# Attention steps taken in pairs, runs in another order, and the instruction order laid out nine times

## The chip, the core and the metric

The kernel runs on one core of one Trainium2 chip. The core has TensorE (matmuls, "PE" in the profile, its weight loads "PEld"), VectorE ("DVE"), ScalarE ("ACT"), GpSimd ("POOL") and SyncE ("SP"), which issues the DMAs. The metric is the device time of one execution in microseconds (us); lower is better.

## The reference

Two layers work on x of shape (2, 1024, 512), all in fp32. Each layer normalises x and adds to it causal attention and a gated feed-forward network of the same normalised input:

```python
for layer in range(2):
    xn = layernorm(x)
    x = x + attention(xn, Wq, Wk, Wv, Wo) + ffn(xn, gate, up, down)
# attention: 16 heads of 32; rotary embedding of q and k (two forms); causal softmax(q k / sqrt(32)) v; then Wo
# ffn: (silu(xn gate) * (xn up)) down, hidden 2048 in layer 0, 1408 in layer 1 (there with scales)
```

## The kernel before, in words

**Phases, groups, runs, steps.** There are four phases, one for each layer and batch entry (2 x 2). In a phase the 16 heads form four groups of four heads. A group has four *runs*, one for each block of 256 queries (`qb` 0 to 3); run `qb` has `qb + 1` *steps*, each over 256 keys. So a group has 10 steps, a phase 40, the kernel 64 runs and 160 steps. Runs go in the order 0, 1, 2, 3 in a group, in the last group of all 3, 2, 1, 0 (`blocks_of`).

**One step.** `Run.scores(n)` makes the scores of four heads with 32-row matmuls (`sc` in the profile), four at a time in the array, into two PSUM tiles of the pool `p_st`, each for two heads. That pool has two buffers, so a step's scores fill all of it. ScalarE copies both to SBUF, scaled (`s<-sc`, 1024 columns each; 768 in a run's last step, which leaves out a masked quarter). In the last step `mask` applies the causal mask on GpSimd. `blocks` takes maxima on VectorE (`rmax`). After a run's last step the maxima are transposed on TensorE (`mtr`), written to DRAM and read back spread over all partitions (`md`, `mb`). Then `subtract` (VectorE), `exps` (ScalarE) and `summed` (GpSimd, or VectorE where the list finds it earlier; into `acc`) work on s. `Run.weighted(n)` multiplies the exponentials with the values, in matmuls with 32 output columns (`av`), `Run.total` sums `acc` with a matmul on ones (`av<-acc,ones`), and `normalise` divides on VectorE.

**Kinds of matmul.** The list of the kernel tells three kinds: "full" (128 rows and 128 columns), "rows" (sc) and "columns" (av and totals). All other matmuls are full: the feed-forward's units (`ux`, `uy`, `uz`), the projections of queries, keys and values (the same names with `_qk` and `_v`), the down and output projections (`d`, `ps_o`), transposes (`tr`). [...]

**The loop.** `two_layers` loops over the steps. Step i makes its scores, then runs full work as "fill" (`Fill.run`: a share in units of 0.86 us worth of matmuls, with maxima and exponentials recorded between its pieces), and last multiplies the exponentials of step i - `LAG` (`LAG` is 5) with the values. A finished run's total follows there or just after the next scores. `weight(i)` shares the fill over the steps. `Fill.choose` picks the next piece of fill by what can start; general PSUM results share three banks (`bank`), some of them held by a unit.

**The order.** Calls such as `nc.vector.tensor_tensor` execute nothing at once: `Schedule.record` books an operation with a modelled cost, its dependencies and a modelled start. At the end `emit` calls `again`, which lays all operations out anew: TensorE goes by *pieces* (groups of matmuls that stay together; `next_piece` may put a later full piece first where the next one would wait more than `WAIT`), other engines take the operation that is due first, and leave themselves idle up to `RESERVE` for one that is due soon. The operations are then issued in that modelled order, and each engine works through its own in order. GpSimd's additions may go to VectorE (`either`).

Every recorded operation has the line of the helper (L275) in the profile, so operations are told apart by tile names.

Of the kernel before, what the change touches and what calls it, by code (L numbers as in the profile page):

```python
# [37 lines left out]
LAG = 5  # L38

# [95 lines left out]

class Op:
    __slots__ = ("eng", "call", "deps", "after", "dur", "lat", "seq", "start", "end", "urgent", "table", "ready", "locks", "either", "out", "mode", "late")
# [14 lines left out]
class Schedule:  # L152
# [81 lines left out]
    def record(self, eng, method, args, kwargs):  # L234
# [12 lines left out]
        op.urgent = eng is not self.tensor and any(i.tile.pool.psum in ("m", "av") for i in ins)  # L247
        op.locks = self.locks(eng, method, ins)

        op.either = None  # L250
        if eng is self.gpsimd and method == "tensor_tensor":
            op.either = self.vector, *self.cost(self.vector, method, args, kwargs, outs, ins)
# [19 lines left out]
        def call():  # L272
            target = getattr(getattr(self.nc, op.eng.name), method)
            get = lambda a: a.real() if isinstance(a, View) else a
            target(*[get(a) for a in args], **{k: get(a) for k, a in kwargs.items()})  # L275
# [72 lines left out]
    def emit(self):  # L348
        while any(eng.waiting for eng in self.engines):
            self.give(None)  # L350
        self.again()
        for op in sorted(self.ops, key=lambda op: (op.start, op.seq)):
            op.call()

    def again(self):
# [3 lines left out]
        ops = sorted(self.ops, key=lambda op: (op.start, op.seq))  # L359
        tensor = [op for op in ops if op.eng is self.tensor]  # L360
# [36 lines left out]
        def soonest(op):  # L397

            at = self.tensor.free
            for o in op.deps:  # L400
                if o.start is None:
# [6 lines left out]

        def next_piece():
# [3 lines left out]
            if soonest(pieces[0][0]) <= free + (1000.0 if apart else self.WAIT):  # L413
                return 0
# [17 lines left out]
        for _ in ops:  # L432
            best = None
            for eng in self.engines:
# [4 lines left out]
                if eng is self.vector:  # L439

                    first = min((u for u, _ in can), default=float("inf"))
                    for op in known[self.gpsimd]:
                        if op.either:
                            u = max(self.ready_on(op, eng), eng.free, self.port - self.PORT)
# [38 lines left out]
            if op.eng is not eng:  # L483
                op.eng, op.dur, op.lat = op.either
                op.locks = True
# [10 lines left out]
def two_layers(ctx: ExitStack, tc: tile.TileContext, x_in, attn_w, ffn_w, ffn_s, rope, out):  # L496
# [416 lines left out]
    class Values(Unit):  # L913
# [6 lines left out]
        def __init__(self, ph, pair, begins):  # L920
            self.ph, self.pair, self.name, self.begins = ph, pair, f"_v{ph}_{pair}", begins
# [247 lines left out]
    class Run:  # L1169
# [10 lines left out]
        def scores(self, n):  # L1180
# [18 lines left out]
            for h2 in range(2):  # L1199
                s = self.s[n, h2] = tp.tile([P, 4, 2, P], F32, tag="s", name=f"s{self.name}_{n}_{h2}")  # L1200
                a = 1 if last else 0
                nc.scalar.activation(
                    s[:, a:], st[h2].rearrange("p j b q -> p b j q")[:, a:], AF.Copy, scale=SCALE
                )
# [69 lines left out]
        def summed(self, n, h2):  # L1274

            e = self.s[n, h2].rearrange("p (k b) j q -> p k b (j q)", k=2)
            last = n == self.steps - 1
            if n == 0:
                self.acc[h2] = acc_p.tile([P, 2, 2 * P], F32, tag=f"acc{h2}", name=f"acc{self.name}_{h2}")
            acc = self.acc[h2]  # L1280
            if n == 0 and last:
                nc.gpsimd.tensor_copy(acc[:, 0], e[:, 1, 0])
                nc.gpsimd.tensor_tensor(acc[:, 1], e[:, 0, 1], e[:, 1, 1], ALU.add)
                return
# [9 lines left out]
        def weighted(self, n):  # L1294
            if n == 0:
# [14 lines left out]
        def total(self):  # L1310

            for j in range(HG):
# [28 lines left out]
    def blocks_of(ph, g):  # L1341

        qbs = list(range(NQB))
        return qbs[::-1] if (ph, g) == (len(phases) - 1, NG - 1) else qbs
# [15 lines left out]
    class Fill:  # L1360
# [67 lines left out]
        def late_output(self, step):  # L1428
            for o in self.outs:
                more = any(d[1] == o[1] and d[3] == o[3] for d in self.downs) or (self.later and o[1] == self.ph)  # L1430
                if o[0] <= step and (step - o[0] >= 8 or not more):
# [64 lines left out]
    def queue_phase(ph):  # L1496
# [4 lines left out]
        for g in range(NG):  # L1501
            if g + 1 < NG:
                fill.qk.append((t0 + g * per_group + 1, QueriesKeys(ph, g + 1, t0 + g * per_group + 2)))
# [4 lines left out]
        for pair in range(2):  # L1508
            begins = t0 + 4 + pair
            fill.qk.append((begins - 1, Values(ph, pair, begins)))  # L1510
# [93 lines left out]
    def weight(i):  # L1604
# [3 lines left out]
        return 1.2 if i % per_phase < 10 else 1.0  # L1608

    ended = None  # L1610
    carried = 0.0
    for i in range(total + LAG):
        ph = min(i // per_phase, len(phases) - 1)
        now[0] = i
        if i % per_phase == 0 and i < total:
# [3 lines left out]
        run, n = steps[i] if i < total else (None, 0)  # L1619
        if run:  # L1620
            while turned.get((ph, run.g)) != 4:
                assert fill.run(i - 1, 5.0)
            run.scores(n)
            if ended and ended.acc:
                ended.total()
        old, m = steps[i - LAG] if i >= LAG else (None, 0)
        if run and n == run.steps - 1:
            run.mask(n)

        if ended:  # L1630
            ended.normalise()
            ended = None

        def exponentials(r, k, h2, sums=True):
            r.subtract(k, h2)
            r.exps(k, h2)
            if sums:
                r.summed(k, h2)
            if h2 == 1:
                spread_maxima()  # L1640

        def late(r, k):

            return k == 0 and r.steps == LAG - 1

        between = []
        if old and late(old, m):
            between += [lambda h2=h2: exponentials(old, m, h2) for h2 in range(2)]
        elif old and m == 0:
            for h2 in range(2):  # L1650
                old.summed(0, h2)
        if run:
            between += [lambda h2=h2: run.blocks(n, h2) for h2 in range(2)]
        if 0 <= i - LAG + 1 < total:
            r, k = steps[i - LAG + 1]
            if not late(r, k):

                between += [lambda h2=h2: exponentials(r, k, h2, k > 0) for h2 in range(2)]
        end = total + LAG if ph == len(phases) - 1 else (ph + 1) * per_phase
        share = fill.left((ph + 1) * per_phase) * weight(i) / sum(weight(j) for j in range(i, end))  # L1660
        goal = share + max(-4.0, min(4.0, carried))
        spent = fill.run(i, goal, between)
        while between:
            between.pop(0)()
        transpose_maxima(True)
        if run and n == run.steps - 1:
            found.append(run)
        carried = goal - spent
        if old:
            while (old.ph, 2 * m + 1) not in v:  # L1670
                spent += fill.run(i, 5.0)
                carried = goal - spent
            tiles = [old.s[m, h2] for h2 in range(2)]
            while i < total and spent - goal < 6.0 and max(nc.settled(t) for t in tiles) > nc.tensor.free + SOON:
                more = fill.run(i, 2.0)
                if not more:
                    break
                spent += more
                carried = goal - spent
            old.weighted(m)  # L1680
            if m == old.steps - 1:
                ended = old

                nc.advance(nc.tensor.free)
                if i + 1 >= total or max(nc.settled(acc) for acc in old.acc) <= nc.tensor.free:
                    old.total()
    ended.normalise()
# [58 lines left out]
```

## Time and profile before

| what | value |
|---|---|
| median of three runs | 1841.15 us (1841.02 to 1841.37) |
| the profiled execution | 1841.55 us; span of its instructions 1839.8 us |
| mean granted TensorE clock | 0.999 |
| table loads on ScalarE (exponential, silu, square root) | 168, 215.5 us |
| evictions of scores `s<-sc` on ScalarE | 192 of 1024 columns, 1020 ns; 128 of 768 columns, 806 ns |
| subtractions `s<-s,mb` of 1024 columns on VectorE | 192, mean 1442 ns |

The profile gives, for each group of instructions, its count, the time it kept its engine busy, the mean of one, and the idle time before it with what ended that. The timeline view lists merged instructions in order of time. TensorE's busy time includes the modelled draining of its pipeline, so a rate is read from the distance of two starts.

### The profile page before, as it was taken

To read this page: it belongs to the slowest core of one execution; us is meant where nothing else is said; L and a number is where in the kernel's file an instruction comes from. 1 tells how busy PE (TensorE), PEld (TensorE's weight loads), DVE (VectorE), ACT (ScalarE), POOL (GpSimd) and SP (SyncE) were. 2 spreads that over 40 slices of the span, in tenths; PEclk is the share of its full clock that TensorE was granted. 3 is DMA by queue.
4 is the path that set the end of the run, shared out by engine and by line. 5 is a ranking of instruction groups with operands and counts; after the bars stand their busy time and mean duration, and the time that the engine had idled before them with its cause. 6 is when DMAs were issued, how large, how long until landed. Compare 5 with 4: busy or idle time off the path is not lost.

```text
span 1839.8 us, 25881 instructions
## 1 busy us (share of the span) xinstructions
PE 1815.6 (99%) x9360; PEld 871.5 (47%) x9360; DVE 1518.3 (83%) x2097; ACT 1049.3 (57%) x1251; POOL 1092.0 (59%) x1025
## 2 busy tenths in 40 slices
PE   7999999999999999999999999999999999999998
PEld 3464444444445644444444455444444465444443
DVE  6766987878888668768688888888989998999898
ACT  3444565556556545545574655575565755665762
POOL 5514865656666235545357684866778764667575
PEclk9999999999999999999999999999999999999999
DMA  5325442222232422222222325222223322221101
GB/s 189 95 82 150 133 148 81 70 75 86 70 115 86 129 80 65 75 74 80 70 95 87 121 75 161 75 75 80 70 78 97 112 77 72 63 76 61 58 32 70
DMA packets 140336, 165.16 MB, mean 90 GB/s; under 512 B 13360, under 2 KB 93488, under 8 KB 140208
## 3 DMA queue, kind: packets, MB, share of 16 engines
q1 hardware_dynamic: 140208, 163.50, 28.4%
q8 instruction: 74, 1.21, 0.3%
q14 instruction: 54, 0.44, 0.1%
HBM read 134.62 MB, written 28.84 MB: 89 GB/s over the span
## 4 chain that ended last, share of the span: by engine, by line
PE 93%; DVE 4%; DMA 1%; ACT 1%; issue 1%; POOL 0%; SPq 0%; DVEq 0%; ACTq 0%; POOLq 0%
PE d L275 24%; PE ux L275 19%; PE uy L275 9%; PE av L275 9%; PE sc L275 8%; PE ux_qk L275 5%; PE uz L275 5%; PE ux_v L275 3%; PE uy_qk L275 3%; DVE s L275 2%; PE uy_v L275 2%; PE ps_o L275 1%; PE uz_qk L275 1%; DVE rmax L275 1%; PE tr L275 1%; PE uz_v L275 1%
## 5 line engine op out<-in xcount | busy, mean ns | idle before, releaser
L275 DVE TENSOR_TENSOR s<-s,mb 128x1024 f32<-128x1024 f32 (+2 forms) x448 | 498.6, 1144 | 10.8 <-DMA mb<-md 10.8
L275 POOL TENSOR_TENSOR acc<-acc,s 128x512 f32<-128x512 f32 (+1 forms) x350 | 447.5, 1299 | 52.3 <-ACT s L275 40.5
L275 ACT ACTIVATE s<-sc 128x1024 f32<-128x1024 f32 (+1 forms) x320 | 284.0, 934 | 242.4 <-PE sc L275 226.2
L275 PE MATMUL d<-wd,hT 128*128 128x512 f32 x864 | 401.3, 594 | 0.1
L275 ACT ACTIVATE s<-s 128x1024 f32<-128x1024 f32 (+1 forms) x320 | 303.5, 970 | 167.1 <-DVE s L275 165.2
L275 DVE TRANSPOSE_TENSOR_REDUCE rmax<-s 128x32 f32<-128x1024 f32 (+1 forms) x320 | 350.8, 1117 | 46.6 <-POOL s L275 25.8
L275 POOL TENSOR_TENSOR acc<-s 128x512 f32<-128x512 f32 (+1 forms) x107 | 137.2, 1292 | 248.8 <-PE av L275 163.9
L275 PEld LDWEIGHTS d<-wd,hT 128*128 128x128 f32 x864 | 161.4, 190 | 192.6 <-issue 183.0
L275 ACT ACT_TABLE_LOAD x168 | 215.5, 1283 | 6.7 <-DVE s L275 3.7
L275 DVE TENSOR_TENSOR x<-d,x 128x512 f32<-128x512 f32 x224 | 151.6, 678 | 75.4 <-PE d L275 74.9
L275 POOL TENSOR_SCALAR_AFFINE_SELECT s<-s 128x512 f32<-128x512 f32 x128 | 97.3, 771 | 127.7 <-ACT s L275 124.5
L275 PE MATMUL av<-s,v 128*32 128x256 f32 (+1 forms) x2560 | 159.1, 365 | 2.1 <-DVE oT L275 1.8
L275 PEld LDWEIGHTS av<-s,v 128*32 128x32 f32 x2560 | 67.5, 109 | 144.0 <-issue 97.9
L275 PE MATMUL ux<-xs,wu 128*128 128x512 f32 x212 | 101.7, 602 | 0.1
L275 PE MATMUL ux<-xs,ws 128*128 128x512 f32 x212 | 101.4, 600 | 0.0
L275 PE MATMUL ux<-xnT,wu 128*128 128x512 f32 x212 | 101.3, 600 | 0.0
L275 PE MATMUL uy<-xnT,ws 128*128 128x512 f32 x212 | 99.7, 593 | 1.0 <-ACT p L275 1.0
L275 PE MATMUL ux<-xnT,wg 128*128 128x512 f32 x212 | 100.7, 597 | 0.0
L275 PE MATMUL d<-wo,oT 128*128 128x512 f32 x194 | 100.2, 598 | 0.0
L275 PE MATMUL uy<-xs,ws 128*128 128x512 f32 x212 | 99.7, 593 | 0.4 <-DVE hT L275 0.4
L275 PE MATMUL uz<-xnT,wg 128*128 128x512 f32 x212 | 99.6, 592 | 0.0
L275 ACT ACTIVATE hT<-hT 128x512 f32<-128x512 f32 x62 | 39.1, 630 | 80.7 <-DVE hT L275 80.4
(191 smaller groups left out, 2529.0 us busy)
## 6 DMA issues: line engine op xcount, KB each, us to landing
mb<-md SPq DMA_DIRECT2D x64, 512.0 KB, 3.8
wg<-in_gate SPq DMA_DIRECT2D x54, 256.0 KB, 2.9
wd<-in_down SPq DMA_DIRECT2D x32, 256.0 KB, 3.1
xr<-xm SPq DMA_DIRECT2D x32, 256.0 KB, 2.7
wu<-in_up SPq DMA_DIRECT2D x28, 256.0 KB, 3.0
s12gu<-ws SPq DMA_DIRECT2D x26, 256.0 KB, 2.0
ws<-s12gu SPq DMA_DIRECT2D x26, 256.0 KB, 2.6
wd<-wds SPq DMA_DIRECT2D x22, 256.0 KB, 3.1
```

The costliest lines, as they stand in the source:

```text
L275: target(*[get(a) for a in args], **{k: get(a) for k, a in kwargs.items()})
```

## The change

**Pairs.** The loop goes over pairs of steps (i - 1, i) with i even. A pair first runs a little more fill, up to 6 units, while the exponentials of the first of its two older steps are not nearly ready; then come the scores of step i - 1, the products for steps i - 6 and i - 5 (with totals of runs that end there, or, where `acc` is not ready, after the next scores), the scores of step i, and then the fill of both steps. Maxima of the two new steps and the exponentials of steps i - 4 and i - 3 are recorded between the pieces of that fill.

**Runs in another order.** 2, 0, 1, 3 in a group, 3, 1, 2, 0 in the last. The one-step run (`qb` 0) takes its product's PSUM tile from the general banks, and its total directly from s, with 8 matmuls (4 of 256 columns, 4 of 128), without `acc` on GpSimd.

**Evictions on either engine.** For the first scores of a pair (`soon`) a `tensor_scalar` on VectorE is booked as an alternative to ScalarE's eviction.

**Layouts.** `best` calls `again` for nine pairs of `RESERVE` and `WAIT` and keeps the layout whose last TensorE operation ends first by the model. `next_piece` looks at when the column matmuls of the whole piece can start, not only its first.

**Due times.** The next group's projections of queries and keys come two steps later and open four steps later (order of runs); those of values are queued at steps 1 and 2 of a phase instead of 3 and 4; late output projections are taken after 5 steps instead of 8.

```diff
+PASSES = [(r, w) for w in (300.0, 150.0, 600.0) for r in (600.0, 300.0, 1200.0)]
...
     def emit(self):
         while any(eng.waiting for eng in self.engines):
             self.give(None)
-        self.again()
+        self.best()
...
+        kept, shortest = state(), None
+        for self.RESERVE, self.WAIT in PASSES:
+            self.again()
+            end = max(op.end for op in self.ops if op.eng is self.tensor)
+            if shortest is None or end < shortest:
+                kept, shortest = state(), end
+            else:
+                restore(kept)
...
+        def piece_soonest(piece):
+
+            at, within, inside = soonest(piece[0]), 0.0, set(piece)
+            for op in piece:
+                if op.mode == "columns" and piece[0].mode != "full":
+                    at = max(at, soonest(op, inside) - within)
+                within += op.dur
+            return at
...
-            if soonest(pieces[0][0]) <= free + (1000.0 if apart else self.WAIT):
+            if piece_soonest(pieces[0]) <= free + (1000.0 if apart else self.WAIT):
...
-                    for op in known[self.gpsimd]:
+                    for op in known[self.gpsimd] + known[self.scalar]:
...
-        def scores(self, n):
+        def scores(self, n, soon=False):
...
+                other = ("tensor_scalar", (dst, src, SCALE, None, ALU.mult), {}) if soon else None
+                nc.record(nc.scalar, "activation", (dst, src, AF.Copy), {"scale": SCALE}, other)
...
         def weighted(self, n):
-            if n == 0:
+            if self.steps == 1:
+                self.av = bank(f"av{self.name}", (P, 2, QB))
+            elif n == 0:
                 self.av = p_av.tile([P, 2, QB], F32, tag="av", name=f"av{self.name}")
...
-        qbs = list(range(NQB))
-        return qbs[::-1] if (ph, g) == (len(phases) - 1, NG - 1) else qbs
+        return [3, 1, 2, 0] if (ph, g) == (len(phases) - 1, NG - 1) else [2, 0, 1, 3]
...
-                fill.qk.append((t0 + g * per_group + 1, QueriesKeys(ph, g + 1, t0 + g * per_group + 2)))
+                fill.qk.append((t0 + g * per_group + 3, QueriesKeys(ph, g + 1, t0 + g * per_group + 6)))
...
+    for pair in range((total + LAG + 1) // 2):
+        i = 2 * pair
...
+        new = [(*steps[k], k) for k in (i - 1, i) if 0 <= k < total]
+        old = [steps[k] for k in (i - LAG - 1, i - LAG) if 0 <= k < total]
...
+            while new and more < 6.0 and settled(tiles) > nc.tensor.free + 1200.0:
+                spent = fill.run(i - 1, 2.0)
...
+        scores(i - 1)
+        sums = []
+        for r, m in old:
+            r.weighted(m)
+            if m == r.steps - 1:
 
                 nc.advance(nc.tensor.free)
+                if r.steps == 1 or not new or settled(r.acc) <= nc.tensor.free:
+                    total_of(r)
+                else:
+                    sums.append(r)
+        scores(i)
+        for r in sums:
+            total_of(r)
```

More of the change, by code (lines that the diff above doesn't have):

```diff
@@ L38 @@
 LAG = 5
+LATE = 1.0
 def ts(n, size):
@@ L133 @@
 SOON = 100.0
+PASSES = [(r, w) for w in (300.0, 150.0, 600.0) for r in (600.0, 300.0, 1200.0)]
 class Op:
-    __slots__ = ("eng", "call", "deps", "after", "dur", "lat", "seq", "start", "end", "urgent", "table", "ready", "locks", "either", "out", "mode", "late")
+    __slots__ = ("eng", "call", "deps", "after", "dur", "lat", "seq", "start", "end", "urgent", "table", "ready", "locks", "either", "own", "how", "out", "mode", "late")
 class Engine:
@@ L232, in locks, with record @@
         return eng is self.vector and method == "tensor_tensor" and not any(i.tile.pool.psum for i in ins)
-    def record(self, eng, method, args, kwargs):
+    def record(self, eng, method, args, kwargs, other=None):
         outs = [a for k, a in kwargs.items() if k == "out" and isinstance(a, View)]
@@ L248, in record @@
         op.locks = self.locks(eng, method, ins)
+        op.own = None
         op.either = None
         if eng is self.gpsimd and method == "tensor_tensor":
-            op.either = self.vector, *self.cost(self.vector, method, args, kwargs, outs, ins)
+            op.either = self.vector, *self.cost(self.vector, method, args, kwargs, outs, ins), True, (method, args, kwargs)
+        elif other:
+            op.either = self.vector, *self.cost(self.vector, other[0], *other[1:], outs, ins), False, other
+        op.how = method, args, kwargs
+        if op.either:
+            op.own = eng, op.dur, op.lat, op.locks, op.how
         op.deps, op.after = [], []
@@ L272, in call @@
         def call():
+            method, args, kwargs = op.how
             target = getattr(getattr(self.nc, op.eng.name), method)
@@ L350, in emit, with best, restore @@
             self.give(None)
-        self.again()
+        self.best()
         for op in sorted(self.ops, key=lambda op: (op.start, op.seq)):
             op.call()
+    def best(self):
+        state = lambda: [(op.start, op.end, op.eng, op.dur, op.lat, op.locks, op.how) for op in self.ops]
+        def restore(kept):
+            for op, s in zip(self.ops, kept):
+                op.start, op.end, op.eng, op.dur, op.lat, op.locks, op.how = s
+        kept, shortest = state(), None
[6 more added lines that the diff above has]
+                restore(kept)
     def again(self):
         ops = sorted(self.ops, key=lambda op: (op.start, op.seq))
+        for op in ops:
+            if op.own:
+                op.eng, op.dur, op.lat, op.locks, op.how = op.own
         tensor = [op for op in ops if op.eng is self.tensor]
@@ L395, in again, with soonest @@
         rest, last = [], []
-        def soonest(op):
+        def soonest(op, inside=()):
             at = self.tensor.free
             for o in op.deps:
+                if o in inside:
+                    continue
                 if o.start is None:
@@ L441, in again @@
                     first = min((u for u, _ in can), default=float("inf"))
-                    for op in known[self.gpsimd]:
+                    for op in known[self.gpsimd] + known[self.scalar]:
                         if op.either:
-                            u = max(self.ready_on(op, eng), eng.free, self.port - self.PORT)
+                            u = max(self.ready_on(op, eng), eng.free, self.port - self.PORT if op.either[3] else 0.0)
                             if u + 200.0 < first and u + op.either[2] < self.can_start(op) + op.lat:
@@ L483, in again @@
             if op.eng is not eng:
-                op.eng, op.dur, op.lat = op.either
-                op.locks = True
+                op.eng, op.dur, op.lat, op.locks, op.how = op.either
             self.begin(op, at)
@@ L918, in two_layers, with __init__ @@
         shared = {}
-        def __init__(self, ph, pair, begins):
-            self.ph, self.pair, self.name, self.begins = ph, pair, f"_v{ph}_{pair}", begins
+        def __init__(self, ph, pair, begins, opens):
+            self.ph, self.pair, self.name, self.begins, self.opens = ph, pair, f"_v{ph}_{pair}", begins, opens
         def quarter(self, c, r):
@@ L1201, in scores @@
                 a = 1 if last else 0
-                nc.scalar.activation(
-                    s[:, a:], st[h2].rearrange("p j b q -> p b j q")[:, a:], AF.Copy, scale=SCALE
-                )
+                src, dst = st[h2].rearrange("p j b q -> p b j q")[:, a:], s[:, a:]
+                other = ("tensor_scalar", (dst, src, SCALE, None, ALU.mult), {}) if soon else None
+                nc.record(nc.scalar, "activation", (dst, src, AF.Copy), {"scale": SCALE}, other)
         def mask(self, n):
@@ L1277, in summed @@
             last = n == self.steps - 1
+            if self.steps == 1:
+                return
             if n == 0:
@@ L1280, in summed @@
             acc = self.acc[h2]
[L1281 to L1284, printed above, removed]
             if n == 0:
@@ L1294, in weighted @@
         def weighted(self, n):
-            if n == 0:
+            if self.steps == 1:
+                self.av = bank(f"av{self.name}", (P, 2, QB))
+            elif n == 0:
                 self.av = p_av.tile([P, 2, QB], F32, tag="av", name=f"av{self.name}")
@@ L1310, in total @@
         def total(self):
+            if self.steps == 1:
+                for k in (1, 0):
+                    off = 1 - k
+                    for j in range(HG):
+                        nc.tensor.matmul(
+                            self.av[j * DH : (j + 1) * DH, 1, off * P :],
+                            ones,
+                            self.s[0, j // 2][:, 2 * k + off : 2 * k + 2, j % 2, :],
+                            start=(k == 1),
+                            stop=(k == 0),
+                        )
+                self.s = self.acc = None
+                return
             for j in range(HG):
@@ L1430, in late_output @@
                 more = any(d[1] == o[1] and d[3] == o[3] for d in self.downs) or (self.later and o[1] == self.ph)
-                if o[0] <= step and (step - o[0] >= 8 or not more):
+                if o[0] <= step and (step - o[0] >= 5 or not more):
                     return o
@@ L1508, in queue_phase @@
         for pair in range(2):
-            begins = t0 + 4 + pair
-            fill.qk.append((begins - 1, Values(ph, pair, begins)))
+            begins = t0 + 2 + 2 * pair
+            fill.qk.append((t0 + 1 + pair, Values(ph, pair, begins, t0 + 4)))
         fill.qk.sort(key=lambda x: x[0])
@@ L1607, in weight, with __init__, __bool__, pop @@
             return 1.5
-        return 1.2 if i % per_phase < 10 else 1.0
-    ended = None
+        w = 1.2 if i % per_phase < 10 else 1.0
+        return w * LATE if i >= per_group and i // 2 % (per_group // 2) == 0 else w
+    class Beside:
+        def __init__(self, things, late):
+            self.things, self.late = things, late
+        def __bool__(self):
+            while self.late and hasattr(self.late[0][0], "mb"):
+                self.things.append(self.late.pop(0)[1])
+            return bool(self.things)
+        def pop(self, n):
+            return self.things.pop(n)
+    def exponentials(r, k, h2):
+        r.subtract(k, h2)
+        r.exps(k, h2)
+        r.summed(k, h2)
+        if h2 == 1:
+            spread_maxima()
+    def maxima(r, n, h2):
+        r.blocks(n, h2)
+        if (n, h2) == (r.steps - 1, 1):
+            found.append(r)
+    def settled(tiles):
+        return max(nc.settled(t) for t in tiles)
+    def total_of(r):
+        r.total()
+        r.normalise()
     carried = 0.0
-    for i in range(total + LAG):
+    end_all = total + LAG - 1
+    for pair in range((total + LAG + 1) // 2):
+        i = 2 * pair
         ph = min(i // per_phase, len(phases) - 1)
         now[0] = i
+        new = [(*steps[k], k) for k in (i - 1, i) if 0 <= k < total]
+        old = [steps[k] for k in (i - LAG - 1, i - LAG) if 0 <= k < total]
         if i % per_phase == 0 and i < total:
@@ L1618, in two_layers @@
             queue_phase(ph)
-        run, n = steps[i] if i < total else (None, 0)
-        if run:
-            while turned.get((ph, run.g)) != 4:
+        for run, _, _ in new:
+            while turned.get((run.ph, run.g)) != 4:
                 assert fill.run(i - 1, 5.0)
[L1623 to L1668, printed above, removed]
-        if old:
[L1670 to L1676, printed above, removed]
-                    break
[L1678 to L1682, printed above, removed]
-                nc.advance(nc.tensor.free)
-                if i + 1 >= total or max(nc.settled(acc) for acc in old.acc) <= nc.tensor.free:
-                    old.total()
@@ L1687, in two_layers @@
-    ended.normalise()
+        for r, m in old:
+            while (r.ph, 2 * m + 1) not in v:
+                spent = fill.run(i, 5.0)
+                assert spent
+                carried -= spent
+        if old:
+            tiles = [r.s[m, h2] for r, m in old[:1] for h2 in range(2)]
+            more = 0.0
+            while new and more < 6.0 and settled(tiles) > nc.tensor.free + 1200.0:
+                spent = fill.run(i - 1, 2.0)
+                if not spent:
+                    break
+                more += spent
+            carried -= more
@@ new lines, in scores @@
+        def scores(k):
+            for run, n, at in new:
+                if at == k:
+                    run.scores(n, bool(old) and at == i - 1)
+                    if n == run.steps - 1:
+                        run.mask(n)
+        scores(i - 1)
+        sums = []
+        for r, m in old:
+            r.weighted(m)
+            if m == r.steps - 1:
+                nc.advance(nc.tensor.free)
+                if r.steps == 1 or not new or settled(r.acc) <= nc.tensor.free:
+                    total_of(r)
+                else:
+                    sums.append(r)
@@ new lines, in two_layers @@
+        scores(i)
+        for r in sums:
+            total_of(r)
+        things, late = [], []
+        first = [[lambda r=r, n=n, h2=h2: maxima(r, n, h2) for h2 in range(2)] for r, n, _ in new]
+        coming = [steps[k] for k in (i - LAG + 1, i - LAG + 2) if 0 <= k < total]
+        for r, k in coming:
+            ops = [lambda r=r, k=k, h2=h2: exponentials(r, k, h2) for h2 in range(2)]
+            if hasattr(r, "mb") and not late:
+                things += ops
+            else:
+                late += [(r, fn) for fn in ops]
@@ new lines, in two_layers @@
+        if late:
+            things = sum(first, []) + things
+        else:
+            things = sum(first[:1], []) + things + sum(first[1:], [])
+        beside = Beside(things, late)
+        if i < end_all:
+            share = sum(weight(j) for j in (i, i + 1) if j < end_all) * fill.left((ph + 1) * per_phase)
+            share /= sum(weight(j) for j in range(i, end_all if ph == len(phases) - 1 else (ph + 1) * per_phase))
+            goal = share + max(-6.0, min(6.0, carried))
+            carried = goal - fill.run(i, goal, beside)
@@ L1688, in two_layers @@
+        while beside:
+            beside.pop(0)()
+        if late:
+            transpose_maxima(True)
+        while beside:
+            beside.pop(0)()
+        assert not late
     now[0] = total + LAG
```

## The prediction

> **What bounds the kernel now.** I read the page's busy table and chain first, then TensorE's timeline around single attention steps, then the score evictions on ScalarE, then busy time by phase.
>
> ```profile
> span 1839.8 us, 25881 instructions
> PE 1815.6 (99%) x9360; PEld 871.5 (47%) x9360; DVE 1518.3 (83%) x2097; ACT 1049.3 (57%) x1251; POOL 1092.0 (59%) x1025
> PE 93%; DVE 4%; DMA 1%; ACT 1%; issue 1%; POOL 0%; SPq 0%; DVEq 0%; ACTq 0%; POOLq 0%
> ```
>
> TensorE (PE) is busy for 99% of the span and carries 93% of the chain that ended last. Only less time on PE shortens this kernel. But busy time includes pipeline drains, so I look at where matmuls start. Columns below: start, length, engine, line, operation, shape, count.
>
> ```profile
> 901.44 1.88 PE L275 MATMUL uy<-xs,ws 128*128 128x512 f32 x4
> 903.25 1.07 PE L275 MATMUL av<-s,v 128*32 128x256 f32 x16
> 904.25 0.94 PE L275 MATMUL sc<-q_1T,k_2T 32*128 32x256 f32 x16
> 905.12 1.98 PE L275 MATMUL ux<-xnT,wu 128*128 128x512 f32 x4
> 906.93 1.88 PE L275 MATMUL uy<-xnT,ws 128*128 128x512 f32 x4
> 908.65 1.88 PE L275 MATMUL ux<-xs,wu 128*128 128x512 f32 x4
> ```
>
> This is one step's excursion from full 128x128 matmuls (kind "full") to 32-column ones (av, "columns"), to 32-row ones (sc, "rows"), and back. Undisturbed, four 512-column instructions take 908.65 - 906.93 = 1.72 us, 0.43 each. The small kinds run four at a time: 16 of 256 columns should take 0.86. Against that, start to start: the last full group 1.81 (+0.09), av 1.00 (+0.14), this last step's shorter sc, 0.64 worked out, 0.87 (+0.22), the first full group afterwards 1.81 (+0.10). So the three changes of kind cost 0.56 us per step in which nothing runs at speed. Over the whole trace the same subtraction leaves 110 us above the streaming time; changes of kind are about 90 of them, real waits about 17 (5 in the first 31 us). A lone sc has its own row early on:
>
> ```profile
> 64.97 1.88 PE L275 MATMUL uy_qk<-xs,ws_qk 128*128 128x512 f32 x4
> 66.78 0.94 PE L275 MATMUL sc<-q_0T,k_0T 32*128 32x256 f32 x16
> 67.64 1.98 PE L275 MATMUL ux_qk<-xnT,wk 128*128 128x512 f32 x4
> 69.47 1.88 PE L275 MATMUL uy_qk<-xnT,ws_qk 128*128 128x512 f32 x4
> ```
>
> 1.81, 0.86 and 1.83 against 1.72, 0.64 and 1.72: 0.42 in all. A lone av likewise: 0.09 + 0.14 + 0.10 = 0.34.
>
> **The change, part by part.** *Pairs.* Today an excursion is full, av, sc, full: 0.56. A pair is full, sc, av (two steps), sc, full: 0.09 + 0.22 + 0.14 + 0.22 + 0.10 = 0.78, in place of 1.12. It saves 0.34. The order sc to av never stands in the trace; sc to a total (also 32 columns) does, and starts as promptly as sc to full, so I price it alike. Of 160 steps, 77 pairs have scores and products: 77 x 0.34 = 26.0. At the ends, where only one exists, before has 1 x 0.56 + 5 x 0.42 + 5 x 0.34 = 4.3 and after 3 x 0.42 + 1 x 0.56 + 2 x 0.34 = 2.5. Saved in all: 27.9 us.
>
> *Totals of the 16 one-step runs.* They are taken from s directly, so GpSimd loses its 32 copies (13.8 us, off the path), and PE's total grows from 0.43 (4 matmuls of 256 columns, each issued twice) to 0.64 (4 more of 128): 16 x 0.21 = +3.4. Their av takes one of the three general banks; between total and the first full product that needs a third bank stand one sc (1.1 us) and four VectorE operations of normalise (0.44 + 0.20 + 0.45 + 0.42 = 1.5), so it may cost some 0.5 a time; Fill.choose prefers work that needs no bank, and I put nothing in the sum and 8 at most.
>
> *The new wait.* Scores fill both PSUM tiles of p_st, so the second scores of a pair must wait for the first's two evictions. Queued behind them in TensorE's order is all full work. The eviction's row:
>
> ```profile
> 1106.25 1.15 PE L275 MATMUL sc<-q_1T,k_0T 32*128 32x256 f32 x16
> 1107.33 1.12 PE L275 MATMUL ps_o<-wo,oT 128*128 128x512 f32 x2
> 1107.51 1.94 ACT L275 ACTIVATE s<-sc 128x1024 f32<-128x1024 f32 x2 [3.46 <-PE sc L275]
> ```
>
> Sc gives way after 1.08 us; its evictions are done 3.20 after its start (a last step's 768 columns: 2.54; sc then gives way after 0.87). Between the two sc lie the two products. A group's ten steps, in the order 2, 0, 1, 3, give five kinds of pair. First scores of step 1 (1024): the products are two full ones, 0.86 + 0.86 + 0.14 = 1.86, so PE is ready at 2.94 and short by 0.3. Step 3 (768): 0.86 + 0.64 + a total 0.43 + 0.14, ready at 2.94, 0.4 to spare. Step 5 (768): ready at 2.73, 0.15 to spare. Step 7 (1024): 0.64 + 0.43 + 0.64 + 0.64 + 0.14, ready at 3.57, 0.35 to spare. Step 9 (768): like step 3. With ScalarE prompt this is 16 x 0.3 = 4.8. The other side: taking all 160 evictions as late as they are today (mean 3.67 and 2.94 after sc starts), the mean wait would be 0.36 a pair, 28 us. Today nothing needs them for a whole step. After, they are due in 3 us, the list leaves an engine idle for work that is soon due, ScalarE is 57% busy, and VectorE may take one of the two (no row has that form; its subtraction on 1024 columns is at least 1.21, an ACT eviction 1.02). I am nearer to the prompt end: +7, bounds 1.5 and 28.
>
> [...]
>
> *The first two full pairs* have scores but no products between: 3.20 - 1.08 = 2.1 and 2.54 - 0.87 = 1.7, +3.9, with nothing to cover it.
>
> *Softmax's time.* A four-step run now has its maximum, subtraction and exponentials for two steps between pair (9, next 0) and the pair that multiplies steps 6 and 7: one pair's work. Before, the product of its first step came 22 to 38 us after its last scores. The subtracting transfer is issued 11 to 19 us after those scores (median 13.6), lands 3.8 later (the page's DMA table), then two subtractions of 1.2 and an exponential of 1.05: 20.9. A group's ten steps take 116 to 139 us in layer 0 (23 to 28 a pair) and 87 to 116 in layer 1 (17.5 to 23). Layer 1 is short by up to 3.5; up to 6 units of 0.86 may be drawn ahead, 5.2, which covers it. Eight such pairs; I take +3, bounds 0 and 16.
>
> *Nine layouts,* the shortest kept: they issue nothing; only the order differs. Of 17 us of waits 12 lie outside the head; I take -3, bounds -8 and 0. Later projections of the next group (two steps) and values are full work moved along PE, at no cost while the 35 us of two pairs that remain cover the rotation; uncovered, the scores wait. Their DMAs and those of the maxima stay in SP's order, where a transfer lands in 2 to 4 us.
>
> Sum: -27.9 + 3.4 + 3.9 + 7 + 3 - 3 = -13.6. The profiled execution took 1841.55 (1.75 around its span), the median is 1841.15; the sum moves the median to **1827.5**. The forecast's own ends: -27.9 + 3.4 + 3.9 + 1.5 - 8 = -27 (1814), and with 15 of waits at the second scores, 8 for softmax and no gain from layouts, +2 (1844).
>
> **The rivals.** *Evictions decide (slower).* The place is the second scores of each pair. At today's lateness 28 stands for my 7: 1827.5 + 21 = 1848.5. It turns the sign where the mean wait passes (7 + 13.6) / 77 = 0.27 us a pair. For: the 3.2 us above against 2.7 to 3.6. Against: 57% of ScalarE. 14%.
>
> *Softmax and VectorE decide.* By phase (the columns as in the page's engines, then clock, DMA):
>
> ```profile
> 43.00:540.00 497.00, 496.97 (x2380) 237.73 (x2379) 389.76 (x542) 263.91 (x321) 285.43 (x280) 1.00 0.33 101
> 1420.00:1798.00 378.00, 374.55 (x2181) 180.79 (x2181) 345.15 (x452) 244.22 (x282) 244.53 (x215) 1.00 0.22 68
> ```
>
> The third figure is VectorE: 78% of the first phase, 91% of the last. Eight layer-1 pairs waiting 2.5 us each: 20 for my 3, 1844.5. A long wait has a second price:
>
> ```profile
> 1433.00:1436.40 3.40, 1.58 (x20) 0.63 (x19) 3.13 (x7) 3.37 (x4) 3.40 (x3) 0.91 0.25 77
> 1436.40:1440.00 3.60, 3.60 (x26) 2.10 (x20) 2.08 (x4) 1.59 (x3) 1.88 (x3) 0.61 0.00 0
> ```
>
> PE was busy 1.58 of 3.40 us, and the granted clock fell to 0.61 after, about 1.4 lost. [...] The 1844.5 holds none of it. 11%.
>
> *The pairs are not kept together:* the layout puts full work between scores and products that are not ready. If half the pairs split, 13 return: 1840.5. For: the list does so already with late totals. Against: piece_soonest looks through the whole piece. 9%.
>
> **How the numbers follow.** Forecast 66%, rivals 14, 11, 9. A measurement can tell about 0.2%, 3.7 us. Faster: nearly all of the forecast and a third of the rivals, 0.75; same 0.06; slower 0.19. The range reaches from the forecast's low end, 1814, to between the two slower rivals, 1846.
>
> **What would show it.** Right: 85 or fewer runs of sc and av among full work, each pair some 0.78 over its streaming time, sc to sc 2.7 to 3.6 us apart, PE's wait for s or sc small, fewer table loads on ScalarE. Wrong: sc to sc beyond 3.9 on average, PE waiting for ACT s near steps 6 and 7 of layer 1, or over 120 excursions.

## The result: slower by 51 us

| kernel | time, median (lowest to highest) | span of the profiled execution | granted clock |
|---|---|---|---|
| before | 1841.26 us (1841.02 to 1843.76) | 1839.8 us | 0.999 |
| after | 1892.36 us (1890.39 to 1893.63) | 1891.9 us | 0.991 |

The ratio is 1.0268 (1.0257 to 1.028, 95%). The profiled execution of after took 1893.63 us. From the page of after, the busy times, the chain that ended last, and three groups (busy us, mean ns of one | idle of the engine before them and what ended it):

```profile
span 1891.9 us, 25904 instructions
PE 1834.5 (97%) x9488; PEld 895.1 (47%) x9488; DVE 1554.7 (82%) x2147; ACT 975.0 (52%) x1165; POOL 1112.3 (59%) x986
PE 73%; DVE 15%; POOL 4%; ACT 3%; issue 2%; DMA 1%; SPq 0%; POOLq 0%; ACTq 0%; DVEq 0%
L288 ACT ACT_TABLE_LOAD x149 | 191.2, 1283 | 5.4 <-DVE s L288 2.7
L288 PE MATMUL av<-s,v 128*32 128x256 f32 (+1 forms) x2560 | 158.8, 368 | 20.4 <-ACT s L288 17.2
L288 DVE TENSOR_SCALAR s<-sc 128x768 f32<-128x768 f32 (+1 forms) x67 | 71.2, 1062 | 16.4 <-PE sc L288 14.9
```

TensorE's share of the chain fell from 93% to 73%; VectorE's rose from 4% to 15%. The products (av) now wait, mostly for the exponentials (ACT s). VectorE took 67 evictions; table loads fell from 168 to 149.

**The pairs are there, at the price foretold.** TensorE's timeline of after:

```profile
131.75 1.88 PE L288 MATMUL uy<-xs,ws 128*128 128x512 f32 x4
133.56 1.15 PE L288 MATMUL sc<-q_1T,k_0T 32*128 32x256 f32 x16
134.64 0.86 PE L288 MATMUL av<-s,v 128*32 128x256 f32 x16
135.31 0.61 PE L288 MATMUL av<-acc,ones 128*32 128x256 f32 x8
135.75 0.83 PE L288 MATMUL av<-s,v 128*32 128x256 f32 x16
136.40 0.83 PE L288 MATMUL av<-s,ones 128*32 128x256 f32 x16
137.16 1.15 PE L288 MATMUL sc<-q_1T,k_0T 32*128 32x256 f32 x16
138.23 1.98 PE L288 MATMUL ux<-xnT,wu 128*128 128x512 f32 x4
140.06 1.88 PE L288 MATMUL uy<-xnT,ws 128*128 128x512 f32 x4
```

From the full group at 131.75 to the one at 140.06 are 8.31 us. The matmuls that start in between, at their undisturbed rates, take 1.72 + 0.86 + 2.36 + 0.86 + 1.72 = 7.52 (2.36 is the four rows of av). So the pair costs 0.79.

**Where the 52 us of span went.** I split TensorE's time between its first and its last matmul, from the distances of starts, in all kernels alike. Streaming is what the matmuls take at their undisturbed rates, changes of kind are priced as in the prediction, lost to half clock is what the granted clock of the windows took, and waits are what then remains. A wait counts to the stretch of one kind that it lengthens, up to the first matmul of the next stretch: of the 32.2 in av and totals, some 6 stand at a stretch's end, nearly all of it before second scores.

| us | streaming | changes of kind | lost to half clock | waits | of these in full work, in sc, in av and totals |
|---|---|---|---|---|---|
| before | 1716.8 | 92.7 | 1.6 | 15.8 | 9.7, 0.2, 5.9 |
| after | 1720.2 | 70.0 | 15.1 | 76.0 | 35.5, 8.3, 32.2 |
| difference | +3.4 | -22.7 | +13.5 | +60.2 | |

These add up to 54.4; the first matmul also starts some 2 to 3 us earlier. The longest waits look like this (TensorE's timeline; in brackets the idle time and what ended it):

```profile
1073.68 0.94 PE L288 MATMUL sc<-q_0T,k_0T 32*128 32x256 f32 x16
1074.55 1.07 PE L288 MATMUL av<-s,v 128*32 128x256 f32 x16
1079.04 2.53 PE L288 MATMUL av<-s,v 128*32 128x256 f32 x16 [3.42 <-ACT s L288]
1081.50 2.09 PE L288 MATMUL sc<-q_0T,k_0T 32*128 32x256 f32 x16
```

and after such a wait the clock is halved (stretch, its length, busy time of PE, PEld, DVE, ACT, POOL, then granted clock, DMA share, GB/s):

```profile
1074.50:1079.00 4.50, 1.12 (x21) 0.42 (x16) 4.23 (x7) 1.66 (x2) 4.01 (x4) 0.88 0.01 2
1079.00:1084.00 5.00, 4.96 (x33) 2.57 (x34) 2.79 (x5) 1.14 (x2) 3.93 (x5) 0.50 0.00 0
```

The 16 products at 1079.04, which take 0.64 to 0.86 elsewhere, take 2.46 to the next start; some of that is the exponential that ends only at 1079.93, the rest the clock. Five such spells (at 64, 1078, 1501, 1621 and 1706 us) make up the loss of after. The first, half as long, follows waits before scores and not before products; run 13 below, in which no wait of products stands among TensorE's waits, loses 1.7 us more to half clock than its control.

**Whom the products wait for.** The chain in order of time at a late pair (start, length, what), that is, the pair (9, next 0) and what follows it:

```profile
1159.59 1.08 PE sc L288 x16
...
1167.44 0.11 PE mtr L288
...
1171.49 4.71 DMA mb<-md
1176.20 0.02 issue
1176.22 6.79 DVE s L288 x4
1183.01 0.02 issue
1183.04 1.07 ACT s L288
```

From the scores at 1159.59 (those of the next run; the four-step run's own last scores start 2.5 us earlier) the chain goes through the transpose of the maxima, the subtracting transfer, **four** subtractions on VectorE and one exponential to the products at 1184.15: 24.6 us. Over all four-step runs, medians from the start of their last scores, layer 0 / layer 1 (steps 6 to 9 of a group are the run's four; fields left empty were not taken):

| us | transfer issued | first subtraction starts | last of four subtractions ends | last exponential of step 7 ends | av of step 6 | av of step 7 |
|---|---|---|---|---|---|---|
| before | 15.2 / 12.5 | | | 33.2 / 29.7 | 34.8 / 28.7 | 46.3 / 37.5 |
| after | 14.8 / 14.5 | 20.5 / 19.6 | 27.2 / 25.6 | 30.2 / 26.9 | 29.9 / 25.4 | 30.8 / 26.3 |

The chain is no slower than before; it is a little quicker. But the products of step 7 used to come 9 to 12 us after those of step 6, and now come 0.9 after. Both steps' exponentials must be done at once, and nothing is left between.

### The profile page after: what moved, and what is told of

Its sections match the earlier page's. It is cut to its first block, busy times and chain, and to the rows that moved or that the text cites. A ratio compares the mean times of both kernels' runs of the same rounds, so it can differ in the third digit from the quotient of the medians.

```text
span 1891.9 us, 25904 instructions
## 1 busy us (share of the span) xinstructions
PE 1834.5 (97%) x9488; PEld 895.1 (47%) x9488; DVE 1554.7 (82%) x2147; ACT 975.0 (52%) x1165; POOL 1112.3 (59%) x986
## 3 DMA queue, kind: packets, MB, share of 16 engines
q1 hardware_dynamic: 140208, 163.50, 27.3%
## 4 chain that ended last, share of the span: by engine, by line
PE 73%; DVE 15%; POOL 4%; ACT 3%; issue 2%; DMA 1%; SPq 0%; POOLq 0%; ACTq 0%; DVEq 0%
PE d L288 20%; PE ux L288 16%; PE uy L288 7%; DVE s L288 6%; PE sc L288 6%; PE av L288 6%; PE ux_qk L288 4%; PE uz L288 4%; POOL acc L288 3%; DVE rmax L288 3%; PE ux_v L288 2%; ACT s L288 2%; PE uy_qk L288 2%; PE ps_o L288 1%; DVE x L288 1%
## 5 line engine op out<-in xcount | busy, mean ns | idle before, releaser
L288 DVE TENSOR_TENSOR s<-s,mb 128x256 f32<-128x256 f32 (+2 forms) x448 | 493.0, 1131 | 9.9 <-DMA mb<-md 9.9
L288 POOL TENSOR_TENSOR acc<-acc,s 128x512 f32<-128x512 f32 (+1 forms) x353 | 457.8, 1318 | 55.6 <-ACT s L288 47.0
L288 POOL TENSOR_TENSOR acc<-s 128x512 f32<-128x512 f32 x96 | 159.7, 1674 | 320.4 <-ACT s L288 219.3
L288 ACT ACTIVATE s<-sc 128x1024 f32<-128x1024 f32 (+1 forms) x253 | 230.6, 945 | 190.7 <-PE sc L288 182.4
L288 PE MATMUL av<-s,v 128*32 128x256 f32 (+1 forms) x2560 | 158.8, 368 | 20.4 <-ACT s L288 17.2
L288 PEld LDWEIGHTS av<-s,v 128*32 128x32 f32 x2560 | 78.2, 111 | 89.7 <-ACT s L288 20.4
L288 PE MATMUL d<-wo,oT 128*128 128x512 f32 x178 | 92.1, 599 | 0.8 <-DVE oT L288 0.4
L288 DVE TENSOR_SCALAR s<-sc 128x768 f32<-128x768 f32 (+1 forms) x67 | 71.2, 1062 | 16.4 <-PE sc L288 14.9
```

## The experiments

Two theories first. **A:** the round trip of a four-step run (maxima, transpose, transfer, subtractions, exponentials) no longer fits into the one pair's fill it has. **B:** TensorE waits for evictions at the second scores, and what follows is late with it. Ratios are to before; brackets give the 95% interval.

**1. No maxima in the subtraction.** The subtraction takes a tile of zeros, so it waits for no transfer; each operation, the transfers too, is still issued. (The pool of `mb` gives one of its two buffers for the zeros.)

```diff
-            m = self.mb[:, h2]
+            m = nomax[:, h2]
```

> The changed kernel, in which the subtraction takes a tile of zeros instead of a run's maxima, so that softmax's maximum is left out; maxima, their transposes and their two transfers are still made, but no exponential waits for them. Theory A (softmax's time: the products of steps 6 and 7 wait for the maxima's round trip, and the waits halve the clock): TensorE's waits before av go (26 us more than in the kernel before), the 13 us at half clock go, and some of the waits behind them: 1825 to 1850 us, against 1892. Theory B (evictions: the second scores of a pair wait for the first's): at most 5 us less, 1887 or more. Theory C (banks, totals and late order of the fill): only the waits before av go, 1855 to 1870.

1833.67 us, 0.9956 (0.9941 to 0.9971): 58.7 less than after. Waits fell from 76.0 to 33.2 (in av and totals from 32.2 to 3.9) and half clock from 15.1 to 1.7. From the page, the busy times and the chain:

```profile
PE 1808.7 (99%) x9488; PEld 891.3 (49%) x9488; DVE 1510.2 (82%) x2116; ACT 1011.8 (55%) x1197; POOL 1131.3 (62%) x1012
PE 88%; DVE 7%; issue 2%; ACT 1%; POOL 1%; DMA 1%; DVEq 0%; POOLq 0%; ACTq 0%
```

VectorE has nearly the same work, 1510 against 1555 us, with 82% of the span in both, and still the loss is gone. So it is the time of the chain, not the load of VectorE. The first products after a late pair now come 25.6 / 19.4 us after the last scores (layer 0 / 1): this is the room that the fill alone gives. Step 7 needs 30.2 / 26.9.

**2. The same in before,** as its control.

> The same edit in the kernel before, as the control: maximum left out of the subtraction, all else still made. Theory A: the kernel before hardly waits for the round trip (6 us of waits before av and totals), so 1 to 9 us less, 1832 to 1840. Theories B and C say the same of it; a fall of 20 or more would mean that the edit helps whatever the order, and would take its force from the first experiment.

1847.38, 1.003 (1.002 to 1.0041): 5 us slower, a miss. The waits in full work rose from 9.7 to 23.6, at units' matmuls that want a copy by VectorE or ScalarE. That exponentials which nothing holds back now go ahead of those copies is my reading, not tested. For the question it does: the transfer costs before nothing, and after 59.

**3. Twice the fill at the late pair.**

```diff
-LATE = 1.0
+LATE = 2.0
```

> The changed kernel with LATE 2.0 for 1.0: pairs after whose scores a four-step run's products come next get twice the share of the fill, so twice the time, at the cost of the four other pairs of a group. Theory A: 8 to 25 us less (1867 to 1884), the waits before av smaller. Theory B: within 4 us of 1892, or slower, since the pairs with least fill get less. Theory C: within 5 us.

1886.71, 1.0243 (1.0225 to 1.0261): only 5.6 less, outside what each of the theories had forecast. The full work between a late pair and the next rose in layer 0, which was less short, from some 25 to some 34 us, but in layer 1 it stayed near 19.5, where it had been. The waits in av and totals rose from 32.2 to 40.7, some 9 of that now at a stretch's end, and half clock fell to 3.3; the idle time of av that the profile puts down to ACT s is 16.4, against 17.2. So this did not give layer 1 the room it was meant to give, and says little on A.

**4. All evictions on ScalarE.**

```diff
-                    run.scores(n, bool(old) and at == i - 1)
+                    run.scores(n, False)
```

> The changed kernel without VectorE as the alternative for the first scores' evictions: ScalarE makes all of them. Theory A: the waits before the second scores grow by 3 to 8 us, the rest stays: 1890 to 1900. Theory B: the evictions are what PE waits for, and all 67 that VectorE took come back: 1905 to 1925.

1892.89, 1.0279 (1.0263 to 1.0294): no change. TensorE's waits (in total, times, longest):

```profile
PE av L288 <- ACT s L288: 15.6, 10, 3.6
...
PE sc L288 <- ACT s L288: 2.4, 4, 1.1
```

The waits in sc did grow, from 8.3 to 19.0, and those in full work and half clock shrank by 11. If evictions made the loss, leaving them one engine would make it larger. It doesn't, so B falls as its cause.

**5 and 6. The maximum of four-step runs over their first three steps,** in after and before: the chain starts at the third step's scores, which in after stand in the pair before, and the last step has no maxima on VectorE.

```diff
+            self.seen = 3 if self.steps == 4 else self.steps
...
-        if (n, h2) == (r.steps - 1, 1):
+        if (n, h2) == (r.seen - 1, 1):
             found.append(r)
```

> The changed kernel, in which a four-step run takes its maximum over its first three steps only (softmax needs any common shift; the last step's maxima are left out), so that the round trip of these runs starts one pair earlier; the other runs are as they were. Theory A (the four-step runs' round trip alone): most of what the first experiment gained, 1836 to 1855. A rival A2 (round trips of all runs, three-step ones too, or exponentials that are late for another reason such as VectorE's load): 1865 to 1885.

> The same edit in the kernel before, as the control. Its four-step runs have three steps' fill between their last scores and their first product, so little waits: by both theories within 6 us of 1842, and 16 runs less two reductions of 0.96 us on VectorE do not count.

After: 1858.15, 1.009 (1.0075 to 1.0105), 34 less. Before: 1844.38, 1.0015 (1.0005 to 1.0024). After lies between the two forecasts, 3 us above A's. One pair's head start in 16 of 64 runs brings two thirds of the loss back.

**7 and 8. The layouts:** nine in before (with the look at the whole piece), one (`RESERVE` 600, `WAIT` 300) in after.

```diff
-        for self.RESERVE, self.WAIT in PASSES:
+        for self.RESERVE, self.WAIT in [(600.0, 300.0)]:
```

> The kernel before with the nine layouts, the shortest kept, and the look at the whole piece, but steps, runs and totals as before (VectorE's alternative is there but no scores ask for it). Forecast term: -3 us, bounds -8 and 0. If the layouts did harm by putting work apart: +5 or more.

> The changed kernel with one layout, RESERVE 600 and WAIT 300 as before the change, in place of the nine. By theory A the layouts hide a few us of waits at best: 1892 to 1903. If the chosen layout was the harm (its RESERVE is 300): 1880 or less.

1841.22, ratio 1.0 (0.9991 to 1.0009), and 1896.69, 1.0301 (1.0277 to 1.0326). So nine layouts are worth nothing before and some 4 us after, at the edge of what the intervals tell.

**9 and 10. Which runs?** First the four-step runs take their maximum over their first step alone; then the other 48 runs do, and the four-step runs over all. Both leave out 96 reductions of maxima: by the profile 107 and 98 us less of them on VectorE.

```diff
+            self.seen = 1 if self.steps == 4 else self.steps
```
```diff
+            self.seen = 4 if self.steps == 4 else 1
```

> The changed kernel, in which the 16 four-step runs take their maximum over their first step only (the other steps' maxima, 96 reductions on VectorE of about 1.1 us, are left out); all other runs are as they were. Theory A (the four-step runs' round trip): these runs can never wait now, and their exponentials spread over earlier pairs, so at or below the fifth experiment's 1858: 1835 to 1858. Theory A2 (round trips of the other runs, or VectorE's load, make the rest): stays at 1858 or above.

> The reverse: the four-step runs take their full maximum, the 48 other runs theirs over the first step only (96 reductions left out, again 110 us of VectorE). Theory A: the wait stays where it is and only VectorE's load falls: 1872 to 1892. Theory A2: as much is gained as in the ninth experiment, 1860 or less.

1844.4, 1.0016 (1.0007 to 1.0025), 48 less than after; and 1879.9, 1.0213 (1.0198 to 1.0228), 12.5 less. In the waits of the second, the products still stand first, and in those of the first they are not among the groups at all:

```profile
PE av L288 <- ACT s L288: 11.9, 6, 7.2
```

VectorE is busy for 80% of the span in both (1480.4 and 1498.8 us), so its relief is nearly the same, and the difference of 35 us belongs to the chain of the four-step runs.

**11 and 12. All runs over their first step alone,** in after and in before.

> The changed kernel with every run's maximum over its first step only (192 reductions left out, some 215 us of VectorE; the shift in softmax is then not always the row's largest score). Theory A: near the first experiment's 1834, 1825 to 1840, as a version that keeps a shift. If VectorE's load had been the bound: well below, 1820 or less.

> The same in the kernel before, as the control for VectorE's 215 us. Theory A: TensorE bound it and hardly waited, so 1832 to 1845. If VectorE's load mattered by itself: 1825 or less.

1839.83, 0.9989 (0.9979 to 0.9999), and 1836.37, 0.9973 (0.9964 to 0.9982). With the chains short in both, after still trails before by 3.5 us.

**13 and 14. No shift at all,** in after and before: maxima, their transposes and transfers and the subtractions are left out. (In exact arithmetic softmax is the same; large scores are not guarded against.)

> The changed kernel with no shift in softmax at all: the maxima, their transposes, both transfers and the subtractions are left out (about 840 us of VectorE and 64 transposes of TensorE, 8 us with their changes). Nothing but evictions, banks and the order of the fill can then delay a pair. Theory A (pairs are worth their changes of kind, 20.6 with totals and head, once softmax keeps up): 15 to 25 us below the fourteenth run, the same kernel without pairs. Theory D (pairing itself costs waits at the second scores and at banks that eat the gain): within 8 us of it.

> The kernel before with no shift in softmax, as the control of the thirteenth run. TensorE bound it, so by both theories it loses its 64 transposes and some waits: 1822 to 1835.

1809.12, 0.9829 (0.9815 to 0.9844), and 1827.69, 0.9928 (0.9912 to 0.9945). Here the change is worth -18.6 us, near its own terms in the prediction, -27.9 + 3.4 + 3.9 = -20.6. Changes of kind went from 91.9 to 64.6 (-27.3), streaming rose by 3.5, waits by 7.2, half clock by 1.7; the first matmul starts 2.6 earlier. VectorE's busy share is 55%:

```profile
PE 1789.8 (99%) x9424; PEld 889.9 (49%) x9424; DVE 996.3 (55%) x1515; ACT 954.9 (53%) x1156; POOL 766.3 (42%) x670
PE 98%; ACT 1%; DVE 1%; DMA 0%; issue 0%; SPq 0%; ACTq 0%
```

So D, the rival named there, falls: the pairs bring what they were priced at, once no run's chain is in their way. VectorE's work has gone with the chains here, so this run does not tell the two apart.

**What the experiments leave.** A is shown: runs 1, 5 and 9 take the loss away by the chain of the four-step runs, run 10 leaves most of it although it relieves VectorE nearly as much, and the controls 2, 6 and 12 move by +5, +2 and -5. Open is why run 1 gains 8.7 us on the runs of before beside it and not 20. Its waits are 33.2 against 15.8, 18.2 of them in full work and 11.1 in sc; with the shift gone altogether they are 17.4 in after and 10.2 in before. A VectorE that is 93% busy in the last phase of run 1 (351.30 of 378.00 us) goes with it, but no run takes that load away with the rest held. Run 11 speaks against the load: VectorE is 85% busy there in the same window (321.13 us), and the same split gives waits of 39.0, against 14.7 in run 12.

## Why the prediction was wrong, step by step

**The failed step: softmax's time.** It stood at +3, with bounds 0 and 16, and rival 2 at 20; waits and half clock rose by 74, of which run 1 shows 56 to hang on the transfer (42.8 of waits, 13.4 of half clock). Three things in its working failed.

*The chain was too short.* I worked out 20.9 us: issue 13.6, landing 3.8, two subtractions, one exponential. That ends at step 6's first half. But a pair multiplies both steps, so the chain ends after four subtractions (6.79 in the chain above, 1.70 each, while I counted two of 1.2) and the last of four exponentials: 26.9 in layer 1. The first subtraction also starts 5 to 5.7 us after the issue, not 3.8. Against the 19.4 us that the fill alone gives, some 7 are missing where I saw up to 3.5.

*"Up to 6 units may be drawn ahead, which covers it" was a loan.* In layer 1 the late pair did get 19.7 us of full work, against 14.5 in run 1; the next pair then had some 10.5, against 12.8 (medians; single ones lie between 5 and 18), since all of it is the same stock. So the products of steps 8 and 9, and those of the next run, wait in their turn. The largest sum by place is the last step (9) of the four-step runs in layer 1: 8.5 us at three places (1501, 1706 and 1788 us). The wait shown at 1079 is of the same step, in the last four-step run of layer 0, with 3.2 more. I priced eight pairs once and let nothing come back later. That these later waits are the loan's is argued: the chain that the profile gives for the one at 1501 has no transfer in it from 1475 us on and goes through GpSimd's sums to an eviction on VectorE, with the subtractions behind it:

```profile
1486.68 3.31 POOL acc L288 x2
1490.06 4.83 POOL acc L288 x4
1494.89 1.27 issue
1496.16 1.45 POOL acc L288
1497.61 0.12 issue
1497.73 0.94 DVE s L288
```

What is shown is that with the chain of the four-step runs out of the way (run 9) no wait of products for exponentials is left among the groups.

*The second price was left out.* I had seen the half clock after a wait, called it 1.4 us and kept it out of the 1844.5. It took 13.5 of the profiled execution by the split. Not all of that is time lost: the three other executions of after have a granted clock of 0.995 in place of 0.991, which is some 6 to 8 us less lost, and are only 0.8 to 3.2 us shorter. In the rows at 1074.50 and 1079.00 TensorE was busy for 1.12 of 4.50 us before the granted clock stood at 0.50, in the row of before for 1.58 of 3.40 us before 0.61: it was not idle throughout in either.

**Right: the price of a pair.** Foretold 0.78; measured 0.785 (exit from full work 0.095, sc 0.22, av 0.149, sc 0.22, back into full work 0.10). The order sc to av costs no more than sc to a total, as assumed.

**Nearly right: changes of kind.** -22.7 for -27.9. Full stretches fell from 169 to 97, where I called for 85 or fewer: totals that were not ready, twelve of them in all, now stand by themselves among full work. In run 1, with 84 stretches, the saving is 25.9. So this is a debt of the same chain.

**Too big: evictions.** I put 7, with bounds 1.5 and 28, and rival 1 at 28. The distances from sc to sc in a pair are, by median, 3.0, 2.52, 2.73, 3.6 and 2.95 for steps 1, 3, 5, 7 and 9; I had worked out 2.94 (short by 0.3), 2.94, 2.73, 3.57 and 2.94. The evictions are in time at these distances. The idle time before sc that the profile puts down to anyone is 7.0 in all: 3.4 to evictions (ACT s and DVE s), where I had 7 and 3.9 for the first two full pairs, and 3.6 to the keys' rotation, which I had put at no cost. Rival 1 falls.

**Right: the totals,** +3.4; in the trace a total's 4 matmuls stand as 8 instructions (`av<-acc,ones` x8), the one-step run's 8 as 16 (`av<-s,ones` x16). **Off: the layouts,** 0 where I had -3 (run 7), though 4 in after (run 8), where there are waits to lay out around. **Rival 2** named mechanism and place. Its price, 20, was made of eight pairs at 2.5 us with nothing given back later and no second price. The sign that I had named for it, TensorE waiting for ACT s near steps 6 and 7 of layer 1, came, but in small part: step 7 waits 2.5 us there in three places, and step 9 the 8.5 above. **Rival 3** falls: the pairs are kept together.

**Open: the rest of the waits in full work.** They rose by 25.8. Run 1 takes 17.3 of that away; the other 8.5 are not explained, and no run tests the general bank that the one-step runs' products now take, for which I had put nothing in the sum and 8 at most.

## What to carry to other kernels

When steps are moved together, follow the longest dependent chain of each kind of run, to its *last* consumer, and compare it with the room left in the shortest phase: the mean load of the engines and a chain's first consumer said nothing here. Independent work drawn ahead to cover a wait is taken from the next one; count where it is missing before calling the wait covered. A saving on the bounding engine that is sure and small (0.34 us, 77 times) was lost here to waits of 3 us in a few places, the more so as the granted clock stood at 0.50 for 6.8 us at four of them.

Of all that was run, run 13 is the fastest, at 0.9829 with the change, ahead of 0.9928 for its control without it; both give up the guard against large scores. The control with first-step maxima, run 12, keeps part of that guard and beats both kernels by little, at 0.9973.

## What the hardware showed that I had not expected

Waits of some 3 us halved the clock for longer than they lasted. At four of them, with TensorE idle for 2.75 to 3.42 us, the granted clock was 0.50 for 6.8 us. The spell began 0.5 to 1.1 us before the wait ended, so TensorE worked through some 6 of the 6.8 us at half speed, and lost about 3. It had not been idle throughout: 1.12 us busy of 4.50 before the spell at 1078, and 1.58 of 4.00 before the one at 1501:

```profile
1497.00:1501.00 4.00, 1.58 (x32) 0.79 (x24) 3.24 (x4) 1.17 (x2) 4.00 (x4) 1.00 0.01 4
1501.00:1505.00 4.00, 2.75 (x20) 1.13 (x24) 2.83 (x4) 1.33 (x2) 3.84 (x4) 0.52 0.00 0
```

Shorter ones mostly left it alone: run 3 has 17 waits of av for ACT s, the longest 2.7 us, and lost 3.3 us to half clock in all.
